# A sandwich layer of attention and experts on one core: other group sizes for the sorted tokens, and another order in the tail

## The chip, the cores and the metric

The program runs on one core of a Trainium2 chip. The core has a matrix engine (TensorE, PE in the profile), a vector engine (VectorE, DVE), an activation engine (ScalarE, ACT), a general engine (GpSimd, POOL) and a queue engine (SyncE, SP) that issues most transfers; each works off its own instructions in order and waits on semaphores for the others. The metric is the device time of one execution in microseconds. The kernel before took 804.39 us, the median of 17 executions between 801.97 and 808.26.

## The reference

The input x has two batches of 2048 tokens with 256 features. Cut to what matters, with normal layer norms without weights unless said:

```python
def _layernorm(x, axis=-1, eps=1e-05):
    m = jnp.mean(x, axis=axis, keepdims=True)
    v = jnp.var(x, axis=axis, keepdims=True)
    return (x - m) / jnp.sqrt(v + eps)
...
xn = layernorm(x, ln_gamma, ln_beta)           # attention, on the normalised x
q, k, v = 4 heads of 64 from xn @ w_q.T, xn @ w_k.T, xn @ w_v.T
qn = rmsnorm(q, q_gamma) * 64 ** -0.5
kn = rmsnorm(k, k_gamma)
attn = softmax(einsum('bhid,bhjd->bhij', qn, kn))
out = einsum('bhij,bhjd->bhid', attn, v) @ w_o.T + b_o
x = x + _layernorm(out)
...
xf = _layernorm(x)                             # experts
chosen = argmax(einsum('bsh,eh->bse', xf, gate_w))       # one of 8
ffn = xf + (expert_w[chosen] @ xf per token)
x = x + _layernorm(ffn)
```

## The kernel before, in words

Tokens lie in tiles of 128, 16 to a batch (NT), 32 in all; all data is float32. First both batches are projected (`project`), then attention runs over 256 steps: batch, block of 512 queries (`qb`, four a batch), pair of heads (`c`, two), tile of keys (`kc`, 16). A step has score matmuls (`s`, line 1049), the exponential on ACT (`p`, 1057), running sums over the keys on DVE (`acc`, 1092 and 1094) and the product with V (`po`, 1103).

The order of the work is written out in Python, and every engine executes in that order. Steps go in pairs, which the text calls slots; there are 128 after a lead-in (`lead`), and slot numbers in the text leave the lead-in out. In slot n the program writes the scores of pair n+1, the sums of pair n, then calls `between(n)`, then writes `po` of pair n. `between` advances generators that are due: all other work is a Python generator, queued with the slot at which it begins and moved on by one `yield` per slot. A generator marked by `early` does its first step ahead of the others of its slot. Steps that yield `later` or nothing wait for the next slot; steps that yield `then` go on at once during attention.

After eight slots a half-block is complete: `oT` is copied from `po`, `block_sums` forms the sums over partitions (`sm`, 1065) and divides on DVE in four quarters (1073, 1074). After sixteen slots the four token tiles of the block follow as `tokens`: the output product `py` (802), a norm with a residual (`x2`), the gate scores and the pick of an expert (833 to 279), and a second norm that gives `x2n`. They begin four slots apart, or in successive slots (`gap = 1`) where they are the last of a group or of all.

Experts are computed for sorted tokens. A group collects a number of token tiles; group A has the 16 of the first batch, group B 12 of the second. When the last tile of a group has its picks, `order(gr)` runs: `rank` matmuls on the picks (588, 589), a first part on DVE that gives each token its place (598 to 637), in the next slot a second part that ends with the one-hot rows `inrow` (640 to 671), and two slots later the matmuls `src` (681), which turn them into lists of tokens (`gr.src`). For T tiles there are T + 7 places of 128 tokens, each with one expert. `order` then queues a generator `places` for each, one per slot, and after them a generator `collect` for each token tile.

A place gathers its rows on the POOL queue (`rows`, 707), loads its expert's weights into one of the `ring` buffers on SP (721), and then, two slots later, transposes (`pt_g`, 729), copies (734), and in the slot after multiplies (`pe`, 739), takes the norm's moments on DVE (387, 389), their root on POOL (383) and the shift on POOL (400), and writes its result to DRAM in the next slot (755, 756). `collect` gathers a tile's results back by position (777) and adds the residual on DVE two slots later (789).

The last four tiles are in no group: the dense path multiplies them with all eight experts (871) and adds up the chosen ones on DVE (886, 888). They run, with all that is left over, after attention. There `finish()` orders the steps as a list planner: each step of a generator names an engine and a cost in microseconds (`Next`), and takes and gives counted resources (`m` for one of three PSUM banks `ps_m`, `s` for one of two large ones, `x` and `f` for buffers). The planner writes next the step with the earliest start; ties go by the order that `opens` or the step gives, then by rank. After attention norms use a square root on ACT (404), a reciprocal on DVE (406) and a shift on DVE (407); two thirds of the places take their moments on DVE and one third on ACT (`norm_on_act`, 414 to 424).

Of the kernel before, what the change touches and what calls it, by code (L numbers as in the profile page):

```python
# [25 lines left out]
def kernel(  # L26
# [16 lines left out]
    nc = tc.nc  # L43
# [238 lines left out]
    def bounded_path():  # L282
# [29 lines left out]

        g_q8 = route.tile([P, 1], F32, tag="g_q8", name="g_q8")
# [3 lines left out]
        col128 = route.tile([P, NT + E], F32, tag="col128", name="col128")  # L317
        token = route.tile([P, NT], F32, tag="token", name="token")
# [263 lines left out]
        def order(gr):  # L582
# [6 lines left out]
            nc.tensor.matmul(ps[:, P : P + T * E], allones, picks, start=True, stop=True)  # L589
            rank = ps[:, : T * E].rearrange("p (t e) -> p t e", e=E)  # L590
            count = ps[:, P : P + T * E].rearrange("p (t e) -> p t e", e=E)

            def te(name):
                return wk.tile([P, NT, E], F32, tag="te", name=f"{name}{n}", bufs=3)[:, :T, :]
# [14 lines left out]
            over = wk.tile([P, E, NT], F32, tag="over", name=f"over{n}", bufs=1)[:, :, :T]  # L609
# [25 lines left out]
            pos = small.tile([P, NT], F32, tag="pos", name=f"posf{n}", bufs=1)[:, :T]  # L635
# [3 lines left out]
            sl = wk.tile([P, NT + E, E - 1], F32, tag="over", name=f"sl{n}", bufs=1)[:, :S, :]  # L639
# [6 lines left out]
            exp = small.tile([P, NT + E], F32, tag="exp", name=f"expf{n}", bufs=1)[:, :S]  # L646
# [3 lines left out]
            ge = wk.tile([P, NT, NT + E], F32, tag="ge", name=f"ge{n}", bufs=1)[:, :T, : S + 1]  # L650
# [6 lines left out]
            tile_1 = small.tile([P, NT], F32, tag="t1", name=f"t1{n}", bufs=1)[:, :T]  # L657
            nc.vector.tensor_reduce(tile_1, ge, AX.X, ALU.add)
            row = small.tile([P, NT], F32, tag="row", name=f"row{n}", bufs=1)[:, :T]
            nc.vector.tensor_scalar(row, tile_1, -float(P), float(P), ALU.mult, ALU.add)  # L660
            nc.vector.tensor_tensor(row, row, pos, ALU.add)
            ids = wk.tile([P, NT, NT + E], F32, tag="ids", name=f"ids{n}", bufs=1)[:, :T, :S]
# [5 lines left out]
            for t in range(0, T, QT4):  # L668
                eq = wk.tile([P, 2 * D], F32, tag="qk", name=f"inrow{n}_{t}", bufs=4)
                inrow.append(eq.rearrange("p (t d) -> p t d", d=P))  # L670
                nc.vector.tensor_tensor(
                    inrow[-1],
                    row[:, t : t + QT4].unsqueeze(2).to_broadcast([P, QT4, P]),
                    col.unsqueeze(1).to_broadcast([P, QT4, P]),
                    ALU.is_equal,
                )
            yield
# [24 lines left out]
        def places(gr, j):  # L702
# [22 lines left out]
            if attending:  # L725
                yield later("PE", 0.3, take="mx", give="mx")
# [69 lines left out]
        def tokens(bt, qb, j, oTs, gr):  # L796
# [27 lines left out]
            scale, _ = yield from norm(y[:, :D], f"z{tt}", away, give="m")  # L824
# [39 lines left out]
            for e in range(E):  # L864
                if e % (HP * EB) == 0:
# [14 lines left out]
                    yield then("DVE", 2.0 if e == 0 else 2.7)  # L880
# [72 lines left out]
        def finish():  # L953
# [33 lines left out]

        opening, gates, order_of = {}, {}, {}
# [131 lines left out]
        for g in range(len(steps) // PAIR):  # L1120
# [414 lines left out]
```

## Time and profile before

| What | Value |
|---|---|
| Median of 17 executions | 804.39 us |
| The profiled execution | 804.73 us |
| its span, first to last instruction | 803.0 us |
| busy: PE / DVE / ACT / POOL | 758.0 / 639.8 / 449.2 / 327.0 us |
| last `po` matmul ends | 723.2 us |
| first dense product starts | 757.5 us |
| last PE instruction ends | 792.4 us |
| granted TensorE clock, mean over the span | 0.982 |

In the profile an instruction is named by engine, line, operation and out<-in with the program's names. A wait is put down to the instruction that released it. PE busy time is modelled, and matmuls overlap their weight loads (PEld), which have rows of their own. Windows give, for a stretch from A to B, its length, then the busy time of PE, PEld, DVE, ACT and POOL with the number of instructions, then the granted clock (1.00 is full speed), the DMA share and GB/s. In rows in order of time the first two numbers are start and duration in us; what stands in brackets is the idle time before and what ended it.

### The profile page before, as it was taken

How to read it: one execution, taken by the hardware profiler on the slowest of the kernel's cores; microseconds unless marked ns; L12 is line 12 of the kernel's file. 1: busy time of each engine (PE TensorE's matmuls, PEld its weight loads, DVE VectorE, ACT ScalarE, POOL GpSimd, SP SyncE). 2: the span in 40 equal slices, each digit the busy share in tenths (PEclk: the TensorE clock that was granted, in tenths of full speed). 3: DMA queues.
4: the chain of work that ended last, by engine and by line, in shares of the span. 5: the costliest groups of instructions: out<-in, count | busy, mean ns of one | idle time of the engine just before them, and what ended most of it. 6: DMA issues, size and time to landing. Idle time of an engine off the chain costs nothing.

```text
span 803.0 us, 10279 instructions
## 1 busy us (share of the span) xinstructions
PE 758.0 (94%) x3169; PEld 317.2 (40%) x3169; DVE 639.8 (80%) x1380; ACT 449.2 (56%) x699; POOL 327.0 (41%) x336
## 2 busy tenths in 40 slices
PE   6999999999999999999997999999999996997794
PEld 4654433433343333333332434444433332334451
DVE  3767678698888879788889967878798899975767
ACT  3666555656565656655654456666656453455751
POOL 4635421144343334242324225757544445127014
PEclk9999999999999999999999999999999998999997
DMA  4100211210100000001221413433212333418326
GB/s 128 54 26 9 72 67 39 67 40 20 40 20 20 20 10 30 8 20 32 84 70 59 126 47 99 131 112 95 64 62 90 105 99 111 128 31 265 84 92 194
DMA packets 48150, 57.58 MB, mean 72 GB/s; under 512 B 5868, under 2 KB 39416, under 8 KB 48088
## 3 DMA queue, kind: packets, MB, share of 16 engines
q1 hardware_dynamic: 41528, 44.65, 17.6%
q0 software_dynamic: 3568, 9.32, 4.7%
q10 hardware_dynamic: 2992, 2.88, 1.2%
q8 instruction: 27, 0.44, 0.2%
q14 instruction: 35, 0.29, 0.1%
HBM read 37.69 MB, written 19.14 MB: 71 GB/s over the span
## 4 chain that ended last, share of the span: by engine, by line
PE 75%; DVE 13%; DMA 4%; ACT 3%; issue 3%; POOL 1%; SPq 0%; DVEq 0%; POOLq 0%; ACTq 0%
PE s L1049 24%; PE po L1103 24%; PE pqk L463 7%; DVE acc L1094 4%; PE pv L472 4%; PE peA L739 3%; PE py L802 3%; PE sm L1065 2%; PE pt_qk L500 2%; PE peB L739 1%; PE pt_x L450 1%; DVE acc L1073 1%; PE pe L871 1%; DMA x<-in_L_attn_x_dram 1%; DMA fgA<-fnA,posA 1%
## 5 line engine op out<-in xcount | busy, mean ns | idle before, releaser
L1057 ACT ACTIVATE p<-s,nbound 128x1024 f32<-128x1024 f32 x256 | 271.1, 1110 | 182.1 <-PE s L1049 182.1
L1094 DVE TENSOR_TENSOR acc<-acc,p 128x1024 f32<-128x1024 f32 x224 | 273.7, 1222 | 11.6 <-ACT p L1057 1.4
L1049 PE MATMUL s<-QT,KT 64*128 64x512 f32 x1024 | 254.7, 615 | 2.3 <-ACT p L1057 2.3
L1103 PE MATMUL po<-p,V 128*64 128x512 f32 x1024 | 251.6, 613 | 0.2 <-ACT oT L1138 0.2
L1049 PEld LDWEIGHTS s<-QT,KT 64*128 64x128 f32 x1024 | 87.9, 186 | 164.9 <-issue 92.0
L1103 PEld LDWEIGHTS po<-p,V 128*64 128x64 f32 x1024 | 64.2, 138 | 129.6 <-issue 127.3
L383 POOL TENSOR_TENSOR rn<-rs_t,mhalf 128x8 f32<-128x8 f32 x32 | 58.8, 1839 | 72.7 <-DVE rs_t L382 72.7
L383 POOL TENSOR_TENSOR roots<-rs_t,mhalf 128x1 f32<-128x1 f32 x32 | 23.9, 748 | 93.2 <-DVE rs_t L382 93.2
L463 PE MATMUL pqk<-wqkT,xnT 128*128 128x512 f32 x128 | 60.8, 598 | 0.6 <-ACT xnT L454 0.6
L383 POOL TENSOR_TENSOR rs_z<-rs_t,mhalf 128x1 f32<-128x1 f32 x28 | 34.8, 1245 | 59.0 <-DVE rs_t L382 58.9
L383 POOL TENSOR_TENSOR rs_y<-rs_t,mhalf 128x1 f32<-128x1 f32 x28 | 32.2, 1149 | 55.7 <-DVE rs_t L382 49.1
L1073 DVE RECIPROCAL acc<-acc 128x128 f32<-128x128 f32 x45 | 42.5, 945 | 0.0
L846 ACT ACTIVATE x2n<-x,shift_y,rs_y 128x256 f32<-128x256 f32 x28 | 16.8, 599 | 44.1 <-POOL shift_y L400 39.3
L707 POOL DMA_INDIRECT rows<-x2nA,srcA x23 | 29.8, 1298 | 24.3 <-DVE srcA L688 18.3
L802 PE MATMUL py<-woT,oT 128*128 128x264 f32 x128 | 35.8, 403 | 1.9 <-ACT spare L749 1.4
L777 POOL DMA_INDIRECT fgA<-fnA,posA x16 | 20.0, 1247 | 37.6 <-DVE rs_t L382 12.0
L1073 DVE RECIPROCAL acc<-sm 128x128 f32<-128x128 f32 x19 | 18.1, 950 | 20.1 <-PE sm L1065 20.1
L472 PE MATMUL pv<-wvT,xnT 128*128 128x264 f32 x128 | 33.7, 386 | 0.0
L383 POOL TENSOR_TENSOR rs_fA<-rs_t,mhalf 128x1 f32<-128x1 f32 x23 | 18.1, 785 | 36.0 <-DVE rs_t L382 35.0
L472 PEld LDWEIGHTS pv<-wvT,xnT 128*128 128x128 f32 x128 | 24.3, 190 | 17.4 <-issue 11.0
L480 ACT COPY qk<-pqk 128x512 f32<-128x512 f32 x32 | 18.8, 588 | 20.4 <-PE pqk L463 20.4
L707 POOL DMA_INDIRECT rows<-x2nB,srcB x19 | 20.9, 1099 | 22.8 <-DVE srcB L688 16.8
(265 smaller groups left out, 924.5 us busy)
## 6 DMA issues: line engine op xcount, KB each, us to landing
ring<-weTd SPq DMA_DIRECT2D x34, 256.0 KB, 2.9
x<-in_L_attn_x_dram SPq DMA_DIRECT2D x8, 512.0 KB, 4.0
xr<-in_L_attn_x_dram SPq DMA_DIRECT2D x28, 128.0 KB, 2.2
fnA<-fA SPq DMA_DIRECT2D x23, 128.0 KB, 2.4
we_raw<-in_L_ffn_expert_w_dram ACTq DMA_DIRECT2D x8, 256.0 KB, 2.7
weTd<-weT SPq DMA_DIRECT2D x8, 256.0 KB, 2.2
x2A<-x SPq DMA_DIRECT2D x16, 128.0 KB, 1.7
fgA<-x2A SPq DMA_DIRECT2D x16, 128.0 KB, 2.0
```

The costliest lines, as they stand in the source:

```text
L383: nc.gpsimd.tensor_tensor(dst, t[:, :n], mhalf[:, :n], ALU.pow)
L463: nc.tensor.matmul(pqk, xnT[:, c, :], wqkT[:, c, :, :].rearrange("p a d -> p (a d)"), start=(c == 0), stop=(c == NCH - 1),)
L472: nc.tensor.matmul(pv[:, :DG], xnT[:, c, :], wvT[:, c, :], start=(c == 0), stop=(c == NCH - 1),)
L707: nc.gpsimd.indirect_dma_start(out=xg, out_offset=None, in_=gr.x2n[:, :], in_offset=bass.IndirectOffsetOnAxis(ap=gr.src[:, j : j + 1], axi ...
L739: nc.tensor.matmul(pe, xT[:, c, :], w[:, c, :], start=(c == 0), stop=(c == NCH - 1))
L777: nc.gpsimd.indirect_dma_start(out=o, out_offset=None, in_=gr.fn[:, :], in_offset=bass.IndirectOffsetOnAxis(ap=gr.pos[:, t : t + 1], axis= ...
L802: nc.tensor.matmul(py, oT[:, bass.ts(j, P)], woT[:, c, :], start=(c == 0), stop=(c == NCH - 1),)
L1049: nc.tensor.matmul(s[:, r, :], bt.KT[rows, c, bass.ts(kc, P)], bt.QT[qb][rows, c, :], start=True, stop=True,)
L1057: nc.scalar.activation(p, s, AF.Exp, bias=nbound)
L1073: nc.vector.reciprocal(acc[:, 0, cols], share[:, cols])
L1094: nc.vector.tensor_tensor(acc, acc, p, ALU.add)
L1103: nc.tensor.matmul(po[r * DH : (r + 1) * DH, :], batches[b].V[:, kc, h * DH : (h + 1) * DH], p[:, r, :], start=(kc == 0), stop=(kc == NT - 1),
```

## The change

Group A gets 20 tiles (`GT = NT + QT4`: the first batch and the first block of the second), group B 8, which makes 27 and 15 places instead of 23 and 19. Tables and work tiles of `order` grow to GT; the count's columns begin at KB // 2 since 160 columns no longer fit beside 128, and a fifth `inrow` tile lies in the buffer `sq`. `oT` has three buffers, not four.

`order` loses one of its two empty slots before `src`. Places follow each other at a pace of 0.8 slot in A and 0.6 in B, and the first comes one slot after `src`. As neither pace is 1, no place waits the additional slot between gather and transposes.

In `finish()` the planner first finds the earliest start, and then, among the steps of that engine that could start within 0.1 us of it, takes the lowest order. Generators whose order is not negative must leave one `m` free. Block sums have order -3, tokens -2, places 0, collects 3; the dense products had order 2 before, and their DVE steps have it now.

In the tail the shift of a place's norm and of a token's first norm (`away`) is computed on GpSimd (`soon=False`), with 0.2 us less planned for DVE.

```diff
+        GT = NT + QT4
-        def norm(src, name, shift=None, give=""):
+        def norm(src, name, shift=None, give="", soon=True):
...
-                yield then("DVE", 0.4)
+                yield then("DVE", 0.4 if soon else 0.2)
                 nc.vector.reciprocal(rs, sd)
-                nc.vector.tensor_scalar(shift, mv[:, 0:1], rs, -1.0, ALU.mult, ALU.mult)
+                eng = nc.vector if soon else nc.gpsimd
+                eng.tensor_scalar(shift, mv[:, 0:1], rs, -1.0, ALU.mult, ALU.mult)
...
-            nc.tensor.matmul(ps[:, P : P + T * E], allones, picks, start=True, stop=True)
+            nc.tensor.matmul(ps[:, KB // 2 : KB // 2 + T * E], allones, picks, start=True, stop=True)
...
-                eq = wk.tile([P, 2 * D], F32, tag="qk", name=f"inrow{n}_{t}", bufs=4)
+                tag, bufs = ("qk", 4) if t < 4 * QT4 else ("sq", 1)
+                eq = wk.tile([P, 2 * D], F32, tag=tag, name=f"inrow{n}_{t}", bufs=bufs)
...
             yield
-            yield
             ps = ps_m(f"src{n}")
...
-            at = now + 1
+            at = now + 1 - gr.pace
             for j in range(S):
-                at += 0.34 if at >= len(steps) // PAIR + lead else 1
+                at += 0.34 if at >= len(steps) // PAIR + lead else gr.pace
...
             yield later("PE", 0.3, 3.0, take="mx")
-            if attending:
+            if attending and gr.pace == 1:
                 yield later("PE", 0.3, take="mx", give="mx")
...
-                scale, shift = yield from norm(f, f"f{n}")
+                scale, shift = yield from norm(f, f"f{n}", soon=False)
...
-            scale, _ = yield from norm(y[:, :D], f"z{tt}", away, give="m")
+            scale, _ = yield from norm(y[:, :D], f"z{tt}", away, give="m", soon=False)
...
-                    yield then("DVE", 2.0 if e == 0 else 2.7)
+                    yield then("DVE", 2.0 if e == 0 else 2.7, order=2)
...
-                best = None
+                could = []
                 for rank, g in enumerate(running + [g for _, g in queue]):
                     step = nexts.get(g) or opening.get(g) or Next("", 0.0)
-                    if any(have[k] < step.take.count(k) for k in step.take):
+
+                    kept = dict(m=order_of.get(g, 0) >= 0)
+                    if any(have[k] < step.take.count(k) + kept.get(k, 0) for k in step.take):
                         continue
...
-                    key = (at, order, rank)
-                    if best is None or key < best[0]:
-                        best = key, g, step
-                (at, *_), g, step = best
+                    could.append(((at, order, rank), g, step))
+
+                (at, *_), _, step = min(could, key=lambda c: c[0])
+                could = [
+                    c for c in could if c[2].engine == step.engine and c[0][0] <= at + SLACK
+                ]
+                (at, *_), g, step = min(could, key=lambda c: (c[0][1], c[0]))
...
+        SLACK = 0.1
...
-        for name, first, n in (("A", 0, NT), ("B", NT, NT - QT4)):
+        for name, first, n, pace in (("A", 0, GT, 0.8), ("B", GT, NT - 2 * QT4, 0.6)):
             groups.append(Group(name, n))
-            groups[-1].first = first
+            groups[-1].first, groups[-1].pace = first, pace
...
-                oT = wk.tile([P, KB], F32, tag="oT", name=f"oT{g}", bufs=4)
+                oT = wk.tile([P, KB], F32, tag="oT", name=f"oT{g}", bufs=3)
                 nc.scalar.copy(oT, po)
-                w = opens(block_sums(g, acc, oT), Next("PE", 1.0, take="m"), 0)
+                w = opens(block_sums(g, acc, oT), Next("PE", 1.0, take="m"), -3)
...
-                        opens(w, Next("PE", 0.5, take="m"), 0, lambda end=end: normed.get(end))
+                        opens(w, Next("PE", 0.5, take="m"), -2, lambda end=end: normed.get(end))
```

More of the change, by code (lines that the diff above doesn't have):

```diff
@@ L316, in bounded_path @@
         col = route.tile([P, P], F32, tag="col", name="col")
-        col128 = route.tile([P, NT + E], F32, tag="col128", name="col128")
-        token = route.tile([P, NT], F32, tag="token", name="token")
+        col128 = route.tile([P, GT + E], F32, tag="col128", name="col128")
+        token = route.tile([P, GT], F32, tag="token", name="token")
         roots = route.tile([P, NTT], F32, tag="roots", name="roots")
@@ L588, in order @@
             nc.tensor.matmul(ps[:, : T * E], before, picks, start=True, stop=True)
-            nc.tensor.matmul(ps[:, P : P + T * E], allones, picks, start=True, stop=True)
+            nc.tensor.matmul(ps[:, KB // 2 : KB // 2 + T * E], allones, picks, start=True, stop=True)
             rank = ps[:, : T * E].rearrange("p (t e) -> p t e", e=E)
-            count = ps[:, P : P + T * E].rearrange("p (t e) -> p t e", e=E)
+            count = ps[:, KB // 2 : KB // 2 + T * E].rearrange("p (t e) -> p t e", e=E)
             def te(name):
-                return wk.tile([P, NT, E], F32, tag="te", name=f"{name}{n}", bufs=3)[:, :T, :]
+                return wk.tile([P, GT, E], F32, tag="te", name=f"{name}{n}", bufs=3)[:, :T, :]
             upto = te("count")
@@ L607, in order @@
                 k *= 2
-            over = wk.tile([P, E, NT], F32, tag="over", name=f"over{n}", bufs=1)[:, :, :T]
+            over = wk.tile([P, E, GT], F32, tag="over", name=f"over{n}", bufs=1)[:, :, :T]
             nc.vector.tensor_tensor(
@@ L634, in order @@
             nc.vector.tensor_tensor(w, w, gr.picks, ALU.mult)
-            pos = small.tile([P, NT], F32, tag="pos", name=f"posf{n}", bufs=1)[:, :T]
+            pos = small.tile([P, GT], F32, tag="pos", name=f"posf{n}", bufs=1)[:, :T]
             nc.vector.tensor_reduce(pos, w, AX.X, ALU.add)
@@ L638, in order @@
             yield
-            sl = wk.tile([P, NT + E, E - 1], F32, tag="over", name=f"sl{n}", bufs=1)[:, :S, :]
+            sl = wk.tile([P, GT + E, E - 1], F32, tag="over", name=f"sl{n}", bufs=1)[:, :S, :]
             nc.vector.tensor_tensor(
@@ L645, in order @@
             )
-            exp = small.tile([P, NT + E], F32, tag="exp", name=f"expf{n}", bufs=1)[:, :S]
+            exp = small.tile([P, GT + E], F32, tag="exp", name=f"expf{n}", bufs=1)[:, :S]
             nc.vector.tensor_reduce(exp, sl, AX.X, ALU.add)
             nc.vector.tensor_copy(gr.exp, exp)
-            ge = wk.tile([P, NT, NT + E], F32, tag="ge", name=f"ge{n}", bufs=1)[:, :T, : S + 1]
+            ge = wk.tile([P, GT, GT + E], F32, tag="ge", name=f"ge{n}", bufs=1)[:, :T, : S + 1]
             nc.vector.tensor_tensor(
@@ L656, in order @@
             )
-            tile_1 = small.tile([P, NT], F32, tag="t1", name=f"t1{n}", bufs=1)[:, :T]
+            tile_1 = small.tile([P, GT], F32, tag="t1", name=f"t1{n}", bufs=1)[:, :T]
             nc.vector.tensor_reduce(tile_1, ge, AX.X, ALU.add)
-            row = small.tile([P, NT], F32, tag="row", name=f"row{n}", bufs=1)[:, :T]
+            row = small.tile([P, GT], F32, tag="row", name=f"row{n}", bufs=1)[:, :T]
             nc.vector.tensor_scalar(row, tile_1, -float(P), float(P), ALU.mult, ALU.add)
             nc.vector.tensor_tensor(row, row, pos, ALU.add)
-            ids = wk.tile([P, NT, NT + E], F32, tag="ids", name=f"ids{n}", bufs=1)[:, :T, :S]
+            ids = wk.tile([P, GT, GT + E], F32, tag="ids", name=f"ids{n}", bufs=1)[:, :T, :S]
             nc.vector.tensor_tensor(ids, ge[:, :, :S], ge[:, :, 1:], ALU.subtract)
```

## The prediction

> **What bounds the kernel now.** I read the page's busy shares and slices first, then the waits of TensorE (PE), then time order around the two places where it stands still, then the tail in windows.
>
> ```profile
> PE 758.0 (94%) x3169; PEld 317.2 (40%) x3169; DVE 639.8 (80%) x1380; ACT 449.2 (56%) x699; POOL 327.0 (41%) x336
> PE   6999999999999999999997999999999996997794
> ```
> PE is the bound, so work moved between stages costs what it saves; only the dips (slices 22, 33, 36 to 40) can give or take time. The waits of PE in 400 to 460 and in 450 to 700 us name the first two:
> ```profile
> PE rankA L588 <- DVE picksA L279: 4.2, 1, 4.2
> PE sm L1065 <- DVE acc L1094: 0.9, 1, 0.9
> ...
> PE rankB L588 <- DVE picksB L279: 5.2, 1, 5.2
> PE s L1049 <- ACT p L1057: 1.8, 1, 1.8
> ```
> Both are the slots in which a group's last four tokens come one per slot and VectorE (DVE) is late with their picks. Time order after order A's first wait (start, duration):
> ```profile
> 441.19 1.99 PE L1049 MATMUL s<-QT,KT 64*128 64x512 f32 x8
> 443.98 0.32 DVE L640 TENSOR_TENSOR slA<-end_A,col 128x161 f32<-128x161 f32 x1
> 444.11 1.08 PE L1065 MATMUL sm<-acc,ones 128*64 128x512 f32 x4 [0.94 <-DVE acc L1094]
> 447.27 2.49 DVE L671 TENSOR_TENSOR inrowA<-rowA,col 128x512 f32<-128x512 f32 x4
> 448.75 3.75 PE L681 MATMUL srcA<-idsA,inrowA 128*128 128x23 f32 x32
> ```
> DVE is behind: it builds `inrow` while PE works off one more slot, and src comes just late enough to find it. The windows (PE, PEld, DVE, ACT, POOL busy, then PE clock) show the clock after the wait and the tail:
> ```profile
> 434.00:436.00 2.00, 2.00 (x8) 0.91 (x8) 1.90 (x3) 0.00 (x0) 1.69 (x2) 0.50 0.28 97
> 753.00:758.00 5.00, 2.06 (x9) 1.29 (x10) 4.50 (x23) 4.38 (x18) 0.00 (x0) 0.94 0.20 69
> 783.00:788.00 5.00, 5.00 (x13) 2.28 (x12) 4.72 (x13) 0.89 (x2) 4.09 (x4) 1.00 0.74 217
> 793.00:798.00 5.00, 0.00 (x0) 0.00 (x0) 4.79 (x15) 0.89 (x2) 1.53 (x2) 0.69 0.68 210
> ```
> The last po ends at 723.2; from there to 803.0 is a tail of 79.8 us, in which the first dense product waits behind the places:
> ```profile
> 757.53 5.22 PE L871 MATMUL pe<-weD,kept 128*128 128x512 f32 x8
> 771.44 20.92 PE L871 MATMUL pe<-weD,kept 128*128 128x512 f32 x48
> ```
>
> **The change, part by part.** The profiled execution took 804.73 us (span 803.0), 0.34 over the median of 804.39; I sum against 804.73.
>
> *Work moved, +12.1.* Slots are 3.79 us bare (s at 699.46, 703.25) and 5.06 with one place (products at 498.80, 503.87), so a place is 1.27 of PE. A gets four more places in attention: 5.1. Group B: before, gathers come in slots 123, 124, 125 of 128 and transposes two slots later, which gives three transposes and two products before the end (712.74, 717.86, 721.00; 716.89, 720.03, as traced). Afterwards src is a slot earlier (120), the first gather comes at 121, then every 0.6 slot (121.0, 121.6, ... 125.8), transposes one slot later: 9 transposes and 7 products. That is 5.5 places more, 7.0. The total of slots (42) and of collects (28) stays.
>
> *Order A with one yield less, +7.9.* src now comes where sm stood, after the s that ends at 443.1, and ahead of sm. DVE's part starts at 443.98 plus 0.85 (five doublings over 160 columns, not four over 128), ge, its reduce and the two ids operations grow from 384 to 560 columns (0.18 each, from 0.55 at 384 and 0.40 at 240), so the first inrow is done at 449.5. PE waits 6.4, not 0.9: +5.5. src has 20 tiles, +0.9 (32 matmuls in 3.75). The wait is longer than the 4.2 that brought the clock to 0.50 (the window above), and there po took 2.87, not 1.94, and rank as much more: +1.5, between 0 (a dip need not follow) and 1.9 (all eight matmuls of a po at half speed).
>
> The Trainium skill's page "TensorE: Matmul & The Clock Gate" (section "Why this matters for your kernels") advises no idle gap over some 3 us, as one window of idle halves the clock; its Part 1 puts a window at 3.4 us, which would make this dip an estimated 1.7 and the whole forecast 801.8. It speaks against this step, and the row at 434 agrees.
>
> *Order B, -3.3.* A's collects came in slots 102 to 117, with their additions on DVE two slots later (641.89 to 688.34, 0.48 each, among the tokens). They now begin at slot 115: five additions and their waits leave DVE ahead of the last pick. The waits there are 1.2 (sm at 642.03), 1.8 and 5.2; at A, without collects, the same four tokens cost 4.2: -4.0, and a shorter dip (0.50 lasts 676 to 682 at B), -1.0. DVE's order is 0.8 shorter in its first part and 1.0 before the first inrow, PE reaches src 10.4 us after rank, DVE needs 13.3: a wait of 2.9 where 0.3 was, +2.6; src four tiles shorter, -0.9. Bounds: -6 if no wait remains, 0 if the collects were not the cause.
>
> *Transposes one slot after the gather, +1.5.* A gather starts 4.6 us after the product before it when no token is in the way (525.01 to 529.57) and 7 to 8 when two norms of a token queue on POOL (514.89 to 523.00). It lands 3.7 later in the middle (2.8 to 6.1). The transposes would come two slots and a product after: 11.1 us, with 1.25 places per slot about 11.7. So only token slots are late, by up to 1.7; four of them at A, each about 0.4, nearly nothing at B (no tokens there, slots of 6 us). Queued behind a late transpose is all of PE: po, then the next s. Bounds: 0, and 9, if each of the 28 slots with places is late by a third of a us.
>
> *The tail, -21.0.* Places left: 8 products, 6 transposes, against 16.5 and 16: 8.6 + 4.2 us of PE, from 58.4 to 45.6. With block sums and tokens first, the chain to the first dense product is sm 2.0, reciprocal and product 1.24, py 1.16, y to mv 1.03, square root 0.3, x2 to the second mv 2.45, root and shift 0.66, x2n 0.60, transposes 0.44, copy 0.37: 10.2, with ten handovers of 0.2 and one reciprocal and one y of neighbours, 14.5 instead of 34.3. Dense takes 64 x 0.436 = 27.9, some 5 of places between, and 8.6 behind (four adds, a norm with its root, ACT's 0.6, a DMA): PE's floor is 56. DVE: busy 54.6 in the tail now; less the norms of eight places (10 stats and 11 roots become 6; 5.9) and four shifts (0.9), plus five more of A's collects (2.2) is 50.0. It starts at 2.2, runs at 95% (14.26 of 15 us in 783 to 798), and 3.9 follow its last instruction (799.1): 58.8. DVE ends last, so 58.8; bounds 56, and 68 at a density of 0.80, between today's 0.72 and that.
>
> *Shifts on POOL, 0 beside what DVE saves above.* A shift is 0.214 on DVE; on POOL 0.26 to 1.1. Away is needed at the token's end only; a place's shift stands before ACT's write, up to 1.3 behind a gather. Cover: dense products; bare, 8 x 1 us.
>
> The page "GPSIMD Engine Reference" (section 4.1) keeps elementwise work on VectorE, as GpSimd is about twice as slow on two inputs; by that a shift would take an estimated 0.43, and the sum would stay.
>
> *The rest, 0.* The larger tables are filled once, on a POOL that is 41% busy. oT's third buffer is free when the fourth token's py is done, three slots (11 us) before its next copy; were it not, ACT would hold the exponentials behind it. A fifth inrow in `sq` waits for nobody, as the projections are over. SP gets the same DMAs; a ring load (2.9) has eight buffers. Keeping one ps_m bank for block sums and tokens slows places, which no longer lead. A's faster pace moves PE work within a full stretch.
>
> Sum: 12.1 + 7.9 - 3.3 + 1.5 - 21.0 = -2.8, so 801.9 for this execution, 801.6 for the median.
>
> **The rivals.** *Faster still:* the tail falls to PE's floor (-2.8), gathers are in time (-1.5) and the dip is missed (-1.5): 795.8. For it: DVE's 4.72 of 5 next to a full PE. Against: DVE is full in the last stretch already.
> *Slower, late gathers:* POOL's gather, two norms and a collect per slot stretch the loop past two slots. Gathers of collects take 1.0 to 1.95 of POOL, and B's slots hold all of these. At the 9 above it adds 7.5 to what I took: 809.1. It decides from 2.8 + 1.5 = 4.3 us in all; against it, POOL idles 1.2 to 2.8 before most norms in 520 to 595.
> *Slower, the tail not dense:* ACT and DVE run in the order of the planner's costs, which today leave PE 10.7 us idle between 723.2 and 758 (summed from windows); at DVE's density of 0.80 the tail takes 68: 810.8.
> *No effect:* removal and new wait cancel; zero lies within the forecast's own range, and the removed yield is seen in the code to move src.
>
> **How the numbers follow.** 0.2% is 1.6 us, about what a measurement here can tell from no change. Forecast 0.42 (798 to 805; 0.30 of it faster, 0.12 same), faster rival 0.20, late gathers 0.22 (0.20 slower, 0.02 same), loose tail 0.16 (0.15 slower, 0.01 same): faster 0.50, same 0.15, slower 0.35. The range runs from 791 (the faster rival, B at its bound, -2.7, and 2 of A's wait hidden) to 813 (the loose tail and 2 of late gathers).
>
> **What the changed profile would show.** Right: PE waits some 6 us for inrowA before src, near 3 for inrowB; a wait for picksB near 4; the last po some 18 us later (741); the first dense product 14 to 16 us after it; DVE full in the tail. Wrong: waits of pt_g for DMA rows in most slots; a dense start over 20 us after the last po; a src that waits for nothing. If DVE catches up sooner than its in-order queue says, the sum falls by up to 7; if the tail is set by ACT, it rises as far as 68 does.

## The result, and the profile after

The changed kernel takes 839.34 us (median of 8 executions, 838.20 to 841.49), the kernel before 804.48 beside it (46 executions): ratio 1.043, interval 1.0412 to 1.0448. It is 4.3% slower where the prediction had 801.6, 0.3% faster, and far above its range of 791 to 813. The profiled execution has a span of 837.9 us, against 803.0.

The page after, its busy times, and of its slices those of PE and of PE's clock:

```profile
PE 768.0 (92%) x3169; PEld 323.0 (39%) x3169; DVE 640.1 (76%) x1373; ACT 443.8 (53%) x670; POOL 341.5 (41%) x364
...
PE   6999999999999999999999987999999987785891
...
PEclk9999999999999999999999987899999997897996
```

The counts show the same work, 3169 matmuls. PE is busy 10 us longer, as more of them ran at a lower clock (mean 0.962, before 0.982). PE's dips up to the last `po` are now slices 24 and 25 (order A) and 33 to 36 (order B and the end of the attention), where the kernel before had 22 and 34 alone. The waits of PE from 387 us to the last `po` (in total, times, longest):

```profile
PE pt_gB L731 <- DMA rows<-x2nB,srcB: 13.0, 3, 5.7
PE rankB L590 <- DVE picksB L279: 5.5, 1, 5.5
PE srcA L683 <- DVE inrowA L674: 5.4, 1, 5.4
PE rankA L590 <- DVE picksA L279: 4.2, 1, 4.2
PE pt_gB L731 <- ACT fB L751: 2.9, 1, 2.9
PE pt_gA L731 <- DMA rows<-x2nA,srcA: 2.6, 2, 1.7
PE srcB L683 <- DVE inrowB L674: 2.5, 1, 2.5
```

The waits for `inrowA` (5.4; 6 was forecast) and `inrowB` (2.5; 3) are there. The one for `picksB` was to fall from 5.2 to 4, and is 5.5. The first line is what the prediction did not have: three waits of the transposes of B's places for their gathered rows.

To see where the 34.9 us lie I matched the exponentials on ACT (the rows `p<-s`) of both traces, in the order in which they come, counted from 130 us on. Up to the 100th, at 388 us, the traces agree to within 1 us. From there the span falls into two parts, the attention up to the end of the last `po`, and the tail (lengths, PE busy and PE idle from windows):

| | attention from exponential 100 | PE busy | PE idle | last `po` ends | tail | PE busy | PE idle | DVE busy |
|---|---|---|---|---|---|---|---|---|
| before | 335.1 | 321.3 | 13.8 | 723.2 | 79.8 | 58.4 | 21.4 | 54.6 |
| after | 382.1 | 345.9 | 36.2 | 769.5 | 68.4 | 44.2 | 24.2 | 49.1 |

The change moved 14.2 us of PE work from the tail into the attention (58.4 to 44.2), about as forecast. But the attention's PE busy time grew by 24.6: some 10 of it are the longer busy time of above. Its idle time grew by 22.4, and the tail's idle time did not fall but rose by 2.8. With 0.7 gained before exponential 100: 24.6 + 22.4 - 14.2 + 2.8 - 0.7 = 34.9.

Most of it comes at the end of the attention. From exponential 222, which comes after `srcB`, to the last `po` the kernel before takes 22.5 us (700.7 to 723.2), the changed one 51.3 (718.2 to 769.5). In order of time, around the first and the last of those waits:

```profile
713.97 1.21 POOL L779 DMA_INDIRECT fgA<-fnA,posA  x1 [6.27 <-DMA out_dram<-fgA]
...
714.80 0.38 SPq L795 DMA_DIRECT2D out_dram<-fgA  x1
...
719.29 1.00 POOL L779 DMA_INDIRECT fgA<-fnA,posA  x1 [4.11 <-DMA ring<-weTd]
720.59 1.53 POOL L709 DMA_INDIRECT rows<-x2nB,srcB  x1 [0.31 <-issue]
...
724.68 0.69 PE L731 MATMUL pt_gB<-ident,rows 128*128 128x128 f32 x2 [5.72 <-DMA rows<-x2nB,srcB]
725.30 3.68 PE L1111 MATMUL po<-p,V 128*64 128x512 f32 x8
...
760.98 1.01 POOL L779 DMA_INDIRECT fgA<-fnA,posA  x1 [5.13 <-DMA out_dram<-fgA]
...
762.29 1.00 POOL L709 DMA_INDIRECT rows<-x2nB,srcB  x1 [0.30 <-issue]
...
765.26 0.66 PE L731 MATMUL pt_gB<-ident,rows 128*128 128x128 f32 x2 [5.40 <-DMA rows<-x2nB,srcB]
765.85 3.68 PE L1111 MATMUL po<-p,V 128*64 128x512 f32 x8
```

In the attention a collect has two `fg` buffers, and one comes free only when the addition two slots later is done and its result is written out. So the gather of a collect of A (line 779) stands in POOL's queue and waits, 6.27 us for `out_dram<-fgA` at 713.97, and the next one another 4.11. The profile puts these 4.11 down to a ring load, which a collect does not use. I take them for the same wait: the result of the collect two before was sent out only at 714.80, and such a write took a median of 3.7 us to land between 700 and 735, which makes 718.5.

The next place's gather (line 709) stands behind this second collect. It follows 0.31 us after the collect has issued, and so lands after PE has come to its transposes. PE waits 5.72, and then runs `po` at half speed (3.68 instead of 1.94). The last wait repeats it, and there the profile names the write: 5.13 of the collect, the place's gather 0.30 behind it, 5.40 of PE.

What stands behind such a wait on PE are the scores of the next slot; without them there is no exponential, no sum on DVE, no addition, and so no free buffer for the next collect. The wait feeds itself: the collect gathered at 724.11 is added only at 739.15. Ahead of its addition on DVE stand a place's moments and the sums of a slot, for which DVE had been idle for 8.25 us up to 732.82.

The page "TensorE: Matmul & The Clock Gate" of the Trainium skill (Part 1, on engine queue depths) states for GpSimd a "per-Q7 strict FIFO", so each of its cores takes its queue in order. The two rows at 719.29 and 720.59 agree.

### The profile page after: what moved, and what is told of

Its sections match the earlier page's. It is cut to its first block, busy times and chain, and to the rows that moved or that the text cites. A ratio compares the mean times of both kernels' runs of the same rounds, so it can differ in the third digit from the quotient of the medians.

```text
span 837.9 us, 10323 instructions
## 1 busy us (share of the span) xinstructions
PE 768.0 (92%) x3169; PEld 323.0 (39%) x3169; DVE 640.1 (76%) x1373; ACT 443.8 (53%) x670; POOL 341.5 (41%) x364
## 4 chain that ended last, share of the span: by engine, by line
PE 73%; DVE 15%; DMA 4%; issue 3%; ACT 2%; POOL 1%; DVEq 0%; SPq 0%; POOLq 0%; ACTq 0%
PE po L1111 24%; PE s L1057 23%; PE pqk L465 7%; DVE acc L1102 4%; PE pv L474 3%; PE py L804 3%; PE peA L741 2%; PE sm L1073 2%; PE pt_qk L502 2%; PE pe L873 2%; PE pt_x L452 1%; DVE acc L1081 1%; PE peB L741 1%; PE srcA L683 1%; DMA rows<-x2nA,srcA 1%
## 5 line engine op out<-in xcount | busy, mean ns | idle before, releaser
L1111 PE MATMUL po<-p,V 128*64 128x512 f32 x1024 | 257.9, 626 | 0.0
L384 POOL TENSOR_TENSOR rs_z<-rs_t,mhalf 128x1 f32<-128x1 f32 x28 | 40.7, 1453 | 96.6 <-DVE rs_t L383 96.6
L804 PE MATMUL py<-woT,oT 128*128 128x264 f32 x128 | 35.8, 403 | 1.5 <-ACT spare L751 1.5
L384 POOL TENSOR_TENSOR rs_fA<-rs_t,mhalf 128x1 f32<-128x1 f32 x27 | 24.0, 889 | 28.8 <-DVE rs_t L383 27.7
L388 DVE BATCH_NORM_STATS2 st_fA<-fA 128x6 f32<-128x256 f32 x27 | 11.5, 424 | 30.8 <-ACT fA L751 30.8
L873 PE MATMUL pe<-weD,kept 128*128 128x512 f32 x64 | 28.1, 595 | 2.3 <-ACT shift_fB L426 1.8
```

The lines of the kernel that those rows point to most:

```text
L384: nc.gpsimd.tensor_tensor(dst, t[:, :n], mhalf[:, :n], ALU.pow)
L804: nc.tensor.matmul(py, oT[:, bass.ts(j, P)], woT[:, c, :], start=(c == 0), stop=(c == NCH - 1),)
L873: nc.tensor.matmul(pes[:, r].rearrange("p e d -> p (e d)"), xT[:, c, :], weD[:, c, e + r * EB : e + (r + 1) * EB, :].rearrange("p e d -> p ...
L1111: nc.tensor.matmul(po[r * DH : (r + 1) * DH, :], batches[b].V[:, kc, h * DH : (h + 1) * DH], p[:, r, :], start=(kc == 0), stop=(kc == NT - 1),
```

## The experiments

Every ratio is to the kernel before, run on the same chip; its median was 812 and 813 us on two of the chips used and 803 and 805 in two rounds on a third, so ratios are compared, not times. Where an expectation gives times, it has 804 for the kernel before.

**Four buffers instead of two**, on the changed kernel: every second collect in the attention uses tiles of the projections, which are idle by then.

```diff
-            if attending:
+            if attending and t % 2:
+                o = wk.tile([P, D], F32, tag="xn", name=f"fo{n}")
+                x2 = wk.tile([P, NCH, P], F32, tag="xnT", name=f"fx{n}").rearrange("p c n -> p (c n)")
+            elif attending:
                 z = wk.tile([P, 2 * D], F32, tag="fg", name=f"fg{n}")
+                o, x2 = z[:, :D], z[:, D:]
```

> The changed kernel, but the collects of a group alternate between the two fg tiles and two more pairs that are free by then (xn, xnT): four buffers, not two. Theory P (in the last eight slots of attention, A's collects stand in GpSimd's queue and wait until the output transfer of two collects earlier has landed, and B's gathers stand behind them): the waits of pt_gB for rows, 13.0 + 2.9 us and their clock dips of 5, fall below 4 us in all, the last po moves from 769 to some 750, the time from 839 to 818-823. Rival G (one slot between gather and transposes is too short, whatever stands in the queue): the waits stay above 10 us, the time at 834-842. Rival O (the missing slot of order alone makes the loss): no change, 837-841.

Measured: ratio 1.0154 (1.0125 to 1.0183) instead of 1.043. The last `po` ends at 751.7 instead of 769.5; the waits for B's rows fall from 13.0 to 2.9. That is theory P's signature, and a little less time than it had (818 to 823 would be 1.017 to 1.024).

**The second slot between gather and transposes back**, on the changed kernel:

```diff
-            if attending and gr.pace == 1:
+            if attending:
                 yield later("PE", 0.3, take="mx", give="mx")
```

> The changed kernel, with the second slot between a place's gather and its transposes put back for both groups. G: the waits of pt_gB for rows vanish, and those of A (2.6 us); two products less come before the end of attention; 816-822. P: the collects still hold up the gathers, but a slot of 5 us more is allowed, so about half of the waits go: 824-832. O: 837-842.

Measured: ratio 1.0166 (1.0133 to 1.0198), last `po` at 754.6, 1.8 of waits for B's rows. By its time this is G's range (816 to 822 would be 1.015 to 1.022), so up to here either a held-up gather or a slot that is too short can be the cause; two runs further below decide it. PE's wait for ACT's `fB` grows from 2.9 to 5.7 here.

**The empty slot before `src` back**, on the changed kernel:

```diff
+            yield
             yield
             ps = ps_m(f"src{n}")
```

> The changed kernel, with the removed empty slot of order put back for both groups. O: srcA and srcB find their inrow, the waits of 5.4 and 2.5 us go and so does the half clock in which srcA took 8.7 instead of 4.7: 9 us at A, 2 at B; B's places start a slot later, which gives 1 to 2 us back in the tail: 828-831 under P and O together, as P's waits stay. If the stall at A were hidden: 838-842.

Measured: ratio 1.0208 (1.0162 to 1.0255); both waits of `src` are gone, while 12.0 us of waits for B's rows stay. It gains more than was expected (828 to 831 would be 1.030 to 1.034): order B takes 3.6 less too, and the stretch behind it 7.2. From exponential 150 to 160, which takes in order A, the windows (length, then busy PE, PEld, DVE, ACT, POOL, then PE's clock) of the changed kernel and of this one are:

```profile
495.50:538.00 42.50, 33.23 (x128) 16.77 (x130) 33.58 (x71) 12.55 (x16) 8.69 (x7) 0.76 0.25 72
```
```profile
495.90:530.50 34.60, 30.59 (x126) 13.73 (x128) 32.80 (x71) 12.12 (x15) 8.05 (x7) 0.80 0.29 88
```

So the missing slot alone costs 7.9 us at order A: 5.3 of idle time (9.3 against 4.0) and 2.6 of slower matmuls.

**The groups of 20 and 8 alone**: the kernel before with the new groups, each place a slot after the other, both empty slots, the old tail and the shifts on DVE; the larger tables and three `oT` stay.

```diff
-        for name, first, n in (("A", 0, NT), ("B", NT, NT - QT4)):
+        for name, first, n, pace in (("A", 0, GT, 1), ("B", GT, NT - 2 * QT4, 1)):
```

> The kernel before with groups of 20 and 8 tiles alone: a pace of one slot, two slots from gather to transposes, both empty slots of order, the old planner, shifts on VectorE. Attention carries four more places (5 us) and the tail four fewer; A's collects reach from slot 122 into the tail. P: GpSimd's queue is shared, but only three of B's places come in attention, with two slots each: 804-812. G and O: no loss from the sizes, 798-804.

Measured: ratio 1.0155 (1.0115 to 1.0194), slower than either side had (812 would be 1.010). The attention ends when it did before, at 722.9, and with less idle time (9.1 instead of 13.8), but the tail takes 99.3. PE's work in it is no more than before (56.7 against 58.4), its idle time is (42.6 against 21.4). B's gathers stand behind A's collects, which wait 4.7 and 5.1 us for a buffer's output at 722 and 730; ten of them are only issued from 734 us on, 1.3 us apart (in the kernel before from 725 on), and PE is busy 17.0 of the first 37.1 us of the tail.

**The new order of the tail alone**: the kernel before with the planner's new rule and orders and the shifts on GpSimd.

```diff
-                    yield then("DVE", 2.0 if e == 0 else 2.7)
+                    yield then("DVE", 2.0 if e == 0 else 2.7, order=2)
...
-                (at, *_), g, step = best
+                (at, *_), g, step = min(could, key=lambda c: (c[0][1], c[0]))
```

> The kernel before (groups of 16 and 12, its own slots) with the new order of the tail and the shifts of the sums' and places' norms on GpSimd; nothing else of the change. My sum put -21.0 us on the tail, of which 12.8 were TensorE work that lies in the attention instead; so the order alone is worth 8.2 us. Theory O (the order pays): the first dense product starts some 15 to 20 us after the last po instead of 34, the tail takes 70 to 73 us instead of 79.8, ratio 0.988 to 0.992. Rival (the order is worth nothing, because what is brought forward leaves the same amount of place work behind it, and the collects end last in both): the tail takes 79 to 81, ratio 0.998 to 1.003, and the idle time of TensorE moves from ahead of the dense products to after them.

Measured: ratio 1.0155 (1.0138 to 1.0172), both theories wrong. The attention is that of before to 0.1 us; the tail takes 90.0 us instead of 79.8. Rows of its end:

```profile
742.14 3.60 PE L874 MATMUL pe<-weD,kept 128*128 128x512 f32 x8
...
782.52 1.13 PE L742 MATMUL peB<-ring,xTB 128*128 128x256 f32 x4 [0.52 <-ACT xTB L737]
...
790.53 1.05 POOL L780 DMA_INDIRECT fgB<-fnB,posB  x1 [3.52 <-DMA fgB<-x2B]
...
804.99 1.07 POOL L780 DMA_INDIRECT fgB<-fnB,posB  x1 [0.30 <-issue]
...
809.02 0.48 DVE L792 SCALAR_TENSOR_TENSOR fgB<-fgB,awayB 128x256 f32<-128x256 f32 x1 [0.37 <-DMA fgB<-fnB,posB]
```

Dense starts 18.9 us after the last `po`, where it took 34.3, as the order says. But it is not dense that ends last: each dense token now comes ahead of places, the last place is multiplied at 782.5, and only when all places of B are written can its 12 collects be gathered, one after the other, from 790.5 to 806.1. PE has nothing left from 783.7 on.

**All shifts back on DVE**, on the changed kernel:

```diff
-                scale, shift = yield from norm(f, f"f{n}", soon=False)
+                scale, shift = yield from norm(f, f"f{n}", soon=True)
...
-            scale, _ = yield from norm(y[:, :D], f"z{tt}", away, give="m", soon=False)
+            scale, _ = yield from norm(y[:, :D], f"z{tt}", away, give="m", soon=True)
```

> The changed kernel with all shifts of norms on VectorE, as before; nothing else. My sum put 0 on their move to GpSimd. Theory: within 3 us of the changed kernel, ratio 1.038 to 1.047. Rival (the shifts of the sums' and places' norms stand behind a collect that waits on GpSimd, and this chain is part of what holds TensorE back): 5 to 12 us faster than the changed kernel, ratio 1.027 to 1.036, with the waits of pt_gB for ACT fB gone.

Measured: ratio 1.0503 (1.0466 to 1.0541), slower still by 0.7%, which neither side had. The last `po` is where it was (769.6), the tail takes 72.6 instead of 68.4. By these two profiles the move of the shifts is worth some 4 us in the tail, where I gave it 0.9; by which wait was not settled.

**Four more buffers for the collects after the attention**, on top of four_buffers:

```diff
-        free = []
+        free, qk_room = [], [0] * 4
...
+                if not free and qk_room:
+                    qk_room.pop()
+                    free.append(wk.tile([P, 2 * D], F32, tag="qk", name=f"fq{n}", bufs=4))
```

> four_buffers (1.0154 of the kernel before) with four more buffers for the collects after the attention (the idle qk tiles). Theory B (in the tail, too, the last collects of B wait for a buffer that A's collects hold): the stretch from TensorE's last matmul to the end, 17.6 us in the changed kernel, falls to 10 to 13, ratio 1.007 to 1.011. Rival (the order of VectorE's queue sets the end, since A's adds stand between the dense adds): the gathers start earlier, the adds don't, and the ratio stays at 1.013 to 1.017.

Measured: ratio 1.0191 (1.0171 to 1.0211), above both forecasts and no gain over four_buffers' 1.0154, though its profiled tail is 64.1 us against 73.6. The two ran on different chips, and the next pair settles it.

**All four cures together** (four buffers, the second slot, the slot before `src`, the buffers after the attention), and then **without one of them**:

> The changed kernel with everything that was found against its waits: four buffers for collects in the attention, four more after it, the slot between the equality tiles and src back, the second slot between gather and transposes back. What stays of the change: groups of 20 and 8, paces 0.8 and 0.6, the new order of the tail, shifts on GpSimd. Theory I (only waits cost; work moved into the attention shortens the tail by as much): TensorE's idle time in the attention is back at some 14 to 18 us, the last po at 740 to 745, the tail 62 to 66 us: 803 to 810 us where the kernel before takes 804, ratio 0.998 to 1.008. Rival (waits for picksB of 5.5 and for ACT's fB of 5.7 stay, and the tail does not pay back what was moved): last po at 748 to 752, tail 68 to 72, ratio 1.010 to 1.020.

Measured: 803.26 us beside 802.86, ratio 0.9999 (0.9982 to 1.0016), as theory I had it. The last `po` ends at 736.7, the tail takes 67.2.

> all_waits_cured (0.9999 of the kernel before) with the two fg buffers for collects in the attention that the changed kernel has, in place of four. Theory P (a collect that waits for its buffer's output DMA holds the place gathers behind it in GpSimd's queue): a wait of 5 to 12 us for B's rows comes back, last po 742 to 749, ratio 1.007 to 1.016. Rival (the second slot between gather and transposes, which wait_back had with 1.8 us of such waits, covers the late gathers alone): ratio 0.999 to 1.004.

Measured: ratio 1.0242 (1.0209 to 1.0275). Two buffers in place of four cost 2.4% by themselves, more than theory P had, and the second slot does not cover it: the rival's 0.999 to 1.004 is out. The waits of POOL and of PE from 690 to 770 us in this kernel, and those of PE in all_waits_cured:

```profile
POOL fgA L783 <- DMA out_dram<-fgA: 15.4, 4, 6.7
...
PE pt_gB L732 <- DMA rows<-x2nB,srcB: 7.0, 1, 7.0
PE rankB L590 <- DVE picksB L279: 5.5, 1, 5.5
```
```profile
PE rankB L590 <- DVE picksB L279: 5.5, 1, 5.5
PE pe L881 <- DVE rs_fB L407: 1.6, 1, 1.6
PE pt_gB L732 <- ACT fB L752: 1.6, 1, 1.6
```

In the stretch from exponential 222 to the last `po` alone, PE waits 13.0 us with two buffers (7.0 for rows, 3.7 for ACT's `xTB`, 2.3 for its `fB`) and 1.6 with four.

> all_waits_cured without the four extra buffers for collects after the attention. Theory B (B's last collects wait for buffers of A's): the attention is unchanged, the tail of 67.2 us becomes 71 to 76, ratio 1.005 to 1.011. Rival (the adds are late by VectorE's order, the buffers are not the limit; the timed runs of tail_buffers and four_buffers, 1.019 and 1.015, were on two chips and do not show a gain): 0.998 to 1.003.

Measured: ratio 1.0006 (0.9989 to 1.0023), tail 68.2 instead of 67.2. These four buffers are worth nothing. They do not end the collects' waiting, though: with them the last two gathers of B stand behind 9.93 us on POOL, without them there are two waits of 5.

The stretch from exponential 222 to the last `po`, by buffers and by slots between gather and transposes, in the runs that have the new pace (before: 22.5 us; slot_back and the cured runs also have both empty slots before `src`):

| | next slot | one slot later |
|---|---|---|
| two buffers | 51.3 (changed kernel), 50.9 (shifts_on_dve), 44.1 (slot_back) | 38.1 (wait_back), 43.5 (cured_but_two_buffers) |
| four buffers | 31.5 (four_buffers), 32.2 (tail_buffers) | 26.9 (all_waits_cured), 28.0 (cured_but_tail_buffers) |

**The rank matmuls later.** With the cures in, PE still waits 4.2 and 5.5 us for picks. I queued each `order` a slot later, in all_waits_cured and in the kernel before:

```diff
-                    queue.append((now, order(gr)))
+                    queue.append((now + 1, order(gr)))
```

> all_waits_cured with the order of each group started one slot later, so that the rank matmuls come a slot after the last pick. Theory W (every wait of TensorE costs its length and the half-speed stretch behind it): the waits for picksA (4.2 us) and picksB (5.5) go, and with them three po of 2.9 to 3.7 us instead of 1.94 behind each of them, some 3 to 4 us; some of it is given back by places that start a slot later. 788 to 795 against 803, ratio 0.983 to 0.991. Rival (VectorE is the limit around the order, and the wait moves to src or to the next po): 0.996 to 1.003.

> The kernel before with the same one edit: the order of each group starts one slot later. Its waits for picksA (4.2) and picksB (5.2) and the dips behind them go: theory W gives 792 to 797 us, ratio 0.985 to 0.992. Rival (the wait moves, VectorE being full): 0.997 to 1.003.

Measured: 0.9998 (0.9984 to 1.0013) and 0.9998 (0.9978 to 1.0019). They say nothing: a chain queued for this slot starts in the next one anyway, and the instructions are the same. They are repeats, and show how closely such repeats agree. The same edit with `now + 2`:

> all_waits_cured with each group's order queued two slots on, which is what it takes for the rank matmuls to come one slot later than now. Theory W (a wait of TensorE costs its length and the half-speed po behind it): the waits for picksA (4.1) and picksB (5.5) go, with some 3 to 4 us of po at half speed; part is given back by places that start a slot later: ratio 0.983 to 0.991. Rival (VectorE is full there, 41.3 of 45 us between 495 and 540, and the wait moves on to src or to the next acc): 0.996 to 1.003.

> The kernel before with the same edit. Theory W: the waits for picksA (4.2) and picksB (5.2) go, ratio 0.985 to 0.992. Rival (the wait moves, or the places of B, a slot later, push as much into the tail): 0.997 to 1.004.

Measured: 1.0087 (1.0061 to 1.0113) and 1.0103 (1.0067 to 1.0140): slower, beyond what the rival had. The waits for picks are down to 0.4 and 0.6 us, and PE waits for ACT instead, 16.4 us in 5. Order A of cured_rank_two_later in order of time:

```profile
516.45 3.09 DVE L674 TENSOR_TENSOR inrowA<-rowA,col 128x512 f32<-128x512 f32 x5
519.46 0.95 DVE L1089 RECIPROCAL acc<-sm 128x128 f32<-128x128 f32 x1
...
520.44 0.48 ACT L1093 COPY acc<-sm 128x384 f32<-128x384 f32 x1 [11.55 <-DVE acc L1089]
520.82 2.12 ACT L1073 ACTIVATE p<-s,nbound 128x1024 f32<-128x1024 f32 x2
...
521.99 3.79 PE L1065 MATMUL s<-QT,KT 64*128 64x512 f32 x8 [7.12 <-ACT p L1073]
```

Order A's second half on DVE (`slA` at 512.4 to the last `inrow` at 519.5) now stands ahead of the reciprocal of the half-block's sums; ACT's copy of these sums waits 11.55 us for it, and behind the copy stand the exponentials, for which the scores wait. PE's wait for picks was the cheaper place for DVE's work to show.

No version was faster than the kernel before.

## Why the prediction was wrong, by its own steps

*The step that failed: "Transposes one slot after the gather, +1.5", with its bounds of 0 and 9.* It counted POOL's busy time and the landing of a gather, with the next place's gather free to issue as its slot comes. It counted a collect in a slot as 1.0 to 1.95 of POOL's work and did not ask what it waits for. The wait was in the trace of before, where collects of A waited for `out_dram<-fgA` too, 8.1 us in 3; no place's gather stood behind them there, and none of PE's waits in the attention from 388 us on is for a gather. The pace and the larger A put both into the same slots. Between the changed kernel and all_waits_cured the stretch differs by 51.3 - 26.9 = 24.4 us, of which the buffers alone, with one slot in between, are 43.5 - 26.9 = 16.6. That it is the buffers is shown by cured_but_two_buffers, which differs from all_waits_cured in nothing else. The two profiled spans are 34.0 apart: 24.4 in this stretch, 7.9 at order A, 3.6 at order B, 1.2 in the tail, and -3.1 in all the rest. The rival "late gathers" named the right place and the sign; its mechanism (POOL too busy) and its price of 9 were not right, and "nearly nothing at B" was wrong where all of it lies.

*Order A with one yield less, +7.9:* right in the wait (5.4, where it had 6.4), too small in what follows. The 7.9 measured above are the missing slot alone, and that they are the same number is luck, as the step also held a larger `src`. Against the kernel before, the same four score blocks, three `po`, `sm` and `src` take 30.2 us (504.35 to 534.57) instead of 18.8 (437.40 to 456.22), 11.4 more: 4.4 of wait, 5.0 of `src` (8.74 against 3.75, at half speed throughout) and 2.0 of `sm` and `po`. The step had 0.9 for `src` and 1.5 for the dip, which it laid on `po` and not on `src`.

*Work moved, +12.1:* right in kind, 14.2 in the changed kernel and 11.6 in all_waits_cured, by the fall of PE's busy time in the tail. What it did not say is that this sum is nothing by itself: in all_waits_cured the attention's PE time rises by 10.4 and the tail's falls by 11.6.

*Order B, -3.3:* not reached. From exponential 210 to 222, which takes in order B, the kernel before takes 39.7 us and the changed one 39.4. With the slot before `src` (slot_back, all_waits_cured, and its variants cured_but_two_buffers, cured_but_tail_buffers and cured_rank_later) it is 35.8 to 35.9: the missing slot cost 3.6, where the step had 2.6, and the rest brought 3.8, where it had 5.9. The reason given for most of it, that A's collects delay the picks, does not hold as a price: in groups_only, where the first collect is gathered only at 704 us, the wait for `picksB` is 1.3 instead of 5.5, and the stretch takes 36.3 all the same.

*The tail, -21.0:* -11.4. The work was counted well (PE 44.2 against 45.6, DVE 49.1 against 50.0). What failed is "runs at 95%", taken from one stretch of 15 us. DVE's busy share of the whole tail is 0.68 before, 0.72 after, 0.75 in all_waits_cured. The rival "the tail not dense" had 68 us, and 68.4 came. PE's idle time in the tail is 21.4 before, 24.2 after and 20.4 with all cures, so nothing shows that the new order shortens it; alone with the shifts, on groups of 16 and 12, it costs 10.2. That the rival's 68 came is a match of the number; its reason, that ACT and DVE follow the planner's costs, was not tested. The term took dense for what ends last. B's collects are. In tail_order_only they wait for B's last place. In the changed kernel the first of them does too (gathered at 804.48, after 3.59 of idle time put down to `fnB<-fB`), and the last waits once more for an `fg` buffer, as the chain that ended last shows (start, duration):

```profile
824.82 0.47 DVE fgA L791
826.07 2.96 DMA out_dram<-fgA
...
829.80 4.00 DMA fgB<-fnB,posB
833.82 0.48 DVE fgB L791
```

The addition at 824.82 stands on DVE behind the dense additions. Four buffers more, given to A's collects first, did not help; why DVE stays at three quarters of the tail in all_waits_cured was not settled.

*Shifts on POOL, 0:* not a loss; the move as a whole looks worth some 4 us. A place's shift took 0.26 on POOL in the tail, not the estimated 0.43, against 0.21 on DVE.

The forecast signs were useful. Of those named as right, the waits for `inrow` came; the last `po` came at 769.5, not 741, and the first dense product 18.0 us after it, not 14 to 16. Of those named as wrong, "waits of pt_g for DMA rows" came true, in five slots and not in most, and the three of B were enough. One reading was off by one: the dips that the prediction calls slices 33 and 36 are 34 and 37 on the page before.

## What to carry to other kernels

When work is moved into a stage, list for each in-order queue every wait of the instructions already there, even those that cost nothing now, and ask what the move puts behind them: here a harmless buffer wait of a few microseconds became 2.4% of the kernel. On an engine as full as PE is here (94%), moved work was a zero sum; a gain must be named as idle time that goes, at a place where the chain that ends last is known. A wait of the bound engine for a second, nearly full engine can be only the place where that engine's work shows; moved elsewhere, it cost more here.

## What the runs showed of the hardware

The clock also fell with no wait before it, at the narrow matmuls of `src`. In slot_back `srcA` is 40 matmuls of 27 columns, PE is busy through all of it, and the clock falls in its midst. Windows of one us (length, PE, PEld, DVE, ACT, POOL, clock):

```profile
516.00:517.00 1.00, 1.00 (x11) 1.00 (x11) 1.00 (x3) 0.00 (x0) 0.00 (x0) 1.00 0.86 268
...
519.00:520.00 1.00, 1.00 (x9) 1.00 (x8) 1.00 (x2) 0.00 (x0) 0.00 (x0) 0.70 0.87 217
520.00:521.00 1.00, 1.00 (x7) 1.00 (x6) 0.90 (x3) 0.78 (x2) 0.00 (x0) 0.50 0.68 244
...
525.00:526.00 1.00, 1.00 (x4) 0.49 (x6) 0.90 (x2) 0.00 (x0) 1.00 (x1) 0.50 0.47 119
526.00:527.00 1.00, 1.00 (x8) 0.45 (x4) 1.00 (x2) 0.29 (x1) 0.69 (x2) 0.89 0.03 12
```

`srcA` took 5.52 us and the `po` behind it 3.68; in groups_only and all_waits_cured, also without a wait, 6.39 and about 3.5. After a wait of 5.4, in the changed kernel, it took 8.74, at half speed throughout.

The smaller groups of the kernel before are not free of it. There `srcA`, 32 matmuls of 23 columns, kept the clock at 1.00 (3.75 us, the `po` behind it 1.94), but in before_rank_later, which has the same instructions, it did not; and `srcB`, 24 of 19 columns, had a slow `po` behind it. First `srcA` of before_rank_later, then `srcB` of before:

```profile
448.15 4.17 PE L681 MATMUL srcA<-idsA,inrowA 128*128 128x23 f32 x32
452.25 3.68 PE L1103 MATMUL po<-p,V 128*64 128x512 f32 x8
```
```profile
693.12 2.85 PE L681 MATMUL srcB<-idsB,inrowB 128*128 128x19 f32 x24
695.91 3.62 PE L1103 MATMUL po<-p,V 128*64 128x512 f32 x8
```

Over all traces in which PE comes to `src` without a wait and at the full clock, the clock fell at it, or within 1 us behind it, in six of six with 40 matmuls, in two of four with 32, in two of three with 24 and in none of six with 16 (1.96 us). So a group of 20 has a price at `src` that a missing slot does not explain, and that the groups of before pay in some traces only. Whether it is the number, the width or the time of the narrow matmuls was not tried.

The section "Why this matters for your kernels" of the Trainium skill's page "TensorE: Matmul & The Clock Gate" advises against idle gaps of PE of over some 3 us. The waits of 4.2 and 5.5 us for picks in the changed kernel agree, with the clock at 0.50 and `po` at 3.68 behind both. The dip in slot_back came with PE busy in every window, which this advice does not cover.

The chips differ: the kernel before took 812.4 and 813.2 us on two of them, and 802.9 and 804.6 in two rounds on a third. The step between chips is over 1%, the one between rounds 0.2%.
